# One residual tile per unit, added to in place, and a reordered opening in a planned macaron block (feed-forward, attention, feed-forward) on one Trainium2 core

## The chip, the cores and the metric

The kernel runs on 1 core of one Trainium2 chip. The metric is device time in microseconds (us) of one execution; lower is better. Times that are compared are medians of several runs. A profiled execution gives the trace: what each engine did and when. The engines are PE (TensorE, matrix products), DVE (VectorE), ACT (ScalarE), POOL (GpSimd) and SP (SyncE, which here only issues DMAs). Each engine executes its own queue of instructions in the order in which they were written; an instruction that waits holds up all behind it on that engine.

## The reference

The input x is 32 sequences of 256 tokens of 128 values. The block is

```python
x = x + 0.5 * ffn(layernorm(x))
x = x + attention(layernorm(x))
x = x + 0.5 * ffn(layernorm(x))
```

`ffn` takes the 256 values [x, -x] through three dense layers of widths 512, 512 and 128; the weights are signs (+1 or -1, from boolean arrays k0, k1, k2), each layer is scaled by a scalar (s0, s1, s2), and the first two are followed by `relu(h) * 2`. `attention` has 16 heads of 8 values: Q, K and V projections with biases, softmax of the scaled scores over the 256 tokens of the sequence, the weighted sum of V, and then a layernorm with gamma and beta of (context + its own input).

## The kernel before, in words

Two sequences make a unit, so there are 16 units of 512 tokens; a half of a unit is one sequence. For each unit the kernel runs `first` (the first feed-forward), `norm_attn` and `project` (layernorm, and Q, K, V), `maxima` and `shift` for each half (scores, whose row maxima DVE takes, are made once; the maxima are then written into Q as additional rows by DMA), `weigh` and `context` for each half (the scores are made again, ACT takes the exponential, PE multiplies by V, the layernorm follows), and `second` (the second feed-forward and the store). The last unit runs `second` by halves. Values that need more than float16 are split in two float16 parts, a high one that ACT writes and a low one that DVE writes (or, as below, ACT and POOL).

None of this is issued in program order. Every operation is recorded as a node with an engine, an estimated cost, the keys that it reads and writes, and a rank, which is the unit's number times UNIT = 16 plus an offset of its stage: B0 for the first feed-forward, BA and BP for the attention's norm and projections, BW for the weighing, B1 for the second feed-forward. `_Plan.simulate` then plays the five engines against each other and gives each free engine the ready node of the lowest rank. On PE, feed-forward nodes may run ahead of the scores by at most SKIP ranks (SKIP0 while the rank is below UNTIL); they are what fills PE between scores. The order that comes out is written as fixed instruction queues. The constants do not change the arithmetic, only that order.

A relief rule: an evacuation of PSUM by DVE may be handed to ACT, which writes a float32 tile `full` (two buffers), and POOL, which finishes it, if DVE is backed up by more than BIAS allows. For the sum at the end of a feed-forward, ACT wrote instead into the destination tile itself.

Tiles that matter here: `x` (the unit's input, 4 buffers), `x1` (after the first feed-forward, 7), `x2` (after attention, 4), `x3` (the result, 2); `vaug` and `ks`, three constant buffers each for V and K, which POOL fills with blanks (`blanks`), the ones in V being a copy of `scale`, known only after `projections` has bounded the weights; `xT`, the normalised and turned input of a feed-forward. A unit below QF is turned by PE and then copied by ACT and DVE (`quick`), the others by a DMA transpose on SP after POOL has normalised them. PSUM has two buffers for scores, one for the context, three for all else.

Lines that the steps below use: 368 (a dense product as one 128-row matmul), 371 (the same as four matmuls of 32 columns), 542/543 (statistics on DVE), 544/546 (variance and its power -0.5 on POOL), 551 (quick normalisation on DVE), 571/572 (the high and low parts of a turned tile), 607/608 (high and low parts after a relu), 610/605 (the relief by ACT and POOL), 660 (the residual sum on DVE), 661/662 (the same on ACT and POOL), 767/778 (scores for the maxima, and the maxima on DVE), 835/847 (scores again, and the exponential on ACT), 817 (the context product), 888 (the sum after attention).

Of the kernel before, what the change touches and what calls it, by code (L numbers as in the profile page):

```python
# [53 lines left out]
PT, NHL, NX, NX1, NX2, NXN = 5, 3, 4, 7, 4, 5  # L55

QF, QK = 1, 1
# [7 lines left out]
B0, BA, BP, BW, BV, B1 = -34, -12.145, -7.563, 13, 4, 42.5  # L65

RUSH, AHEAD = 0.302, 5.298

SKIP0, SKIP, UNTIL = 30.226, 7.856, 12.452

WAIT = 0.101
# [3 lines left out]
TURN = 0.1  # L75
# [4 lines left out]
BIAS = 0.471  # L80
# [18 lines left out]
class _Node:  # L99
    __slots__ = ("n", "eng", "cost", "emit", "rank", "kind", "rows", "lag", "needs", "then", "bufs", "count", "avail", "start", "tiling", "alt")  # L100


class _Plan:
# [11 lines left out]
    def op(self, eng, cost, emit, r=(), w=(), rank=0.0, kind="D", rows=0, lag=None, alt=None):  # L115
# [3 lines left out]
        x.then, x.avail, x.start = [], 0.0, None  # L119
# [25 lines left out]
    def simulate(self):  # L145

        free = [0.0] * 5
# [6 lines left out]
        heapq.heappush(events, (0.0, 0, None))  # L154
# [94 lines left out]
        def relief(now, best):  # L249

            nonlocal left
            for x in sorted((x for x in ready[DVE] if x.alt and x.avail <= now + 1e-9), key=lambda x: (x.rank, x.n)):
# [9 lines left out]
                y.n, y.eng, y.cost, y.emit, y.rank, y.kind, y.rows, y.lag, y.alt, y.tiling = x.n, ACT, act, evict, x.rank, "D", 0, None, None, "D"  # L262
                y.needs, y.then, y.bufs, y.count, y.avail, y.start = [], [x], [source, temp], 0, 0.0, None
# [21 lines left out]
        while left:  # L285
# [8 lines left out]
            while again:  # L294
                again = False
                for eng in range(5):
                    if free[eng] > now + 1e-9 or not ready[eng] and eng != ACT:
                        continue
                    if eng == PE:
                        group = choose(now)  # L300
                    else:
                        can = [x for x in ready[eng] if x.avail <= now + 1e-9 and fits(x)]
                        best = min(can, key=lambda x: (x.rank, x.n)) if can else None
                        if eng == ACT:
                            best = relief(now, best) or best
                        group = [best] if best else None
                    if group:
                        begin(group, now)
                        again = True
# [28 lines left out]
def tile_macaron(ctx: ExitStack, tc: tile.TileContext, x, Wq, bq, Wk, bk, Wv, bv, gamma, beta, k0, k1, k2, s0, s1, s2, out):  # L338
# [50 lines left out]
    op(ACT, 0.25, lambda: nc.scalar.copy(ident16, ident), r=["ident"], w=["ident16"], rank=-500)  # L389

    def weights():
# [11 lines left out]
        op(ACT, 0.53, lambda: nc.scalar.dma_start(out=k0s.t, in_=k0.rearrange("(c p) f -> p c f", p=P)), w=[k0s], rank=-900, lag=3.2)  # L403
        for i, src in enumerate((s0, s1, s2)):
            op(SP, 0.47, lambda i=i, src=src: nc.sync.dma_start(out=raw[:, i : i + 1], in_=src.partition_broadcast(P)),
               w=[("raw", i)], rank=-899, lag=2.6)
        op(ACT, 0.53, lambda: nc.scalar.dma_start(out=k1s.t, in_=k1.rearrange("(c p) f -> p c f", p=P)), w=[k1s], rank=-899, lag=4.2)
        op(ACT, 0.53, lambda: nc.scalar.dma_start(out=k2s.t, in_=k2.rearrange("(c p) f -> p c f", p=P)), w=[k2s], rank=-898, lag=4.6)
        raws = [("raw", i) for i in range(3)]
        v = lambda cost, emit, r, w: op(DVE, cost, emit, r=r, w=w, rank=-800)  # L410
# [3 lines left out]
        v(0.6, lambda: nc.vector.tensor_tensor(kd.t, k0s.t[:, 0, :], k0s.t[:, 1, :], ALU.subtract), [k0s], [kd])  # L414
# [10 lines left out]
        v(0.4, lambda: nc.vector.tensor_scalar(w2, k2s.t, 2.0, -1.0, ALU.mult, ALU.add), [k2s], ["w2"])  # L425
        v(0.1, lambda: nc.vector.tensor_tensor(sab, raw, sgn, ALU.mult), [*raws, "sgn"], ["sab"])
        v(0.1, lambda: nc.vector.tensor_tensor(fac, sab[:, 0:1], sab[:, 1:2], ALU.mult), ["sab"], ["fac"])
        v(0.1, lambda: nc.vector.tensor_tensor(fac, fac, raw[:, 2:3], ALU.mult), ["fac", *raws], ["fac"])
        v(0.1, lambda: nc.vector.tensor_scalar(fac, fac, 8.0, None, ALU.mult), ["fac"], ["fac"])
# [9 lines left out]
    def projections():  # L439
# [16 lines left out]
        v = lambda cost, emit, r, w, rank=-600: op(DVE, cost, emit, r=r, w=w, rank=rank)  # L456
# [20 lines left out]
        for i in range(2):  # L477
            op(POOL, 0.5, lambda i=i: permute(br[:, i, 1, :], br[:, i, 0, :], nc.gpsimd.tensor_copy), r=[("br", i)], w=[("brp", i)], rank=-590)
        op(PE, 0.2, lambda: nc.tensor.transpose(bp.t, bound, ident), r=["bound", "ident"], w=[bp], rank=B0 + 2.1)
        v(0.2, lambda: nc.vector.tensor_reduce(top[:, 0:1], bp.t, AX.X, ALU.max), [bp], ["top"])  # L480
        v(0.1, lambda: nc.vector.tensor_scalar(top[:, 1:2], top[:, 0:1], 320.0, 1e-30, ALU.mult, ALU.max), ["top"], ["top"])
        op(POOL, 0.5, lambda: nc.gpsimd.tensor_tensor(top[:, 2:3], top[:, 1:2], nhalf[0:3, 0:1], ALU.pow), r=["top", "nhalf"], w=["top"], rank=-600)
# [3 lines left out]
        op(PE, 0.2, lambda: nc.tensor.matmul(sp.t, ones, diag, start=True, stop=True), r=["ones", "diag"], w=[sp], rank=B0 + 2.2)  # L486
        v(0.1, lambda: nc.vector.tensor_scalar(scale, sp.t, 2.0**13, None, ALU.mult), [sp], ["scale"])
        for i in range(3):
            op(ACT, 0.22, lambda i=i: nc.scalar.activation(ws[:, i, :], ws[:, i, :], AF.Identity, scale=scale[:, i : i + 1]), r=[("ws", i), "scale"], w=[("ws", i)], rank=-600)
# [9 lines left out]
        op(PE, 0.7, turn, r=[*wss, "ident", ("brp", 0), ("brp", 1), "ones"], w=[pw], rank=B0 + 2.3)  # L499
        for i in range(2):  # L500
            op(ACT, 0.4, lambda i=i: permute(wT[:, i, :], pw.t[:, i, :], nc.scalar.copy), r=[pw], w=[("wT", i)], rank=-600)
        op(ACT, 0.22, lambda: nc.scalar.copy(wT[:, 2, :], pw.t[:, 2, :]), r=[pw], w=[("wT", 2)], rank=-600)
        v(0.1, lambda: nc.vector.tensor_tensor(bs, pw.t[:, 3, 0:2], scale[:, 0:2], ALU.mult), [pw, "scale"], ["bs"])
        wTs = [("wT", i) for i in range(3)]
        op(ACT, 0.4, lambda: nc.scalar.copy(wqkv[:, :, 0, :], wT), r=wTs, w=["wqkv0"], rank=-600)
# [9 lines left out]
    def blanks():  # L515
        for j in range(NV):
            rank = -500 if j == 0 else (j - 1) * UNIT * 0.5
# [8 lines left out]
        op(POOL, 0.95, lambda: nc.gpsimd.memset(zero.t.bitcast(F32), 0.0), w=[zero], rank=-501)  # L526
        op(SP, 0.4, lambda: nc.sync.dma_start(out=nought, in_=zero.t), r=[zero], w=["nought"], rank=-500, lag=2)
# [31 lines left out]
    def turned(xn, tag, name, n, rank, quick):  # L559
# [3 lines left out]
        if quick:  # L563
            pt = psum([P, n * P], f"t{name}")

            def turn():
                for t in range(n):
                    nc.tensor.transpose(pt.t[:, bass.ts(t, P)], xn.t[:, t, :], ident)

            op(PE, 0.11 * n, turn, r=[*xns, "ident"], w=[pt], rank=rank)  # L570
            op(ACT, 0.1 * n + 0.1, lambda: nc.scalar.copy(xT.t[:, 0, :], pt.t), r=[pt], w=[(xT, 0)], rank=rank)
            op(DVE, 0.15 * n, lambda: nc.vector.tensor_tensor(xT.t[:, 1, :], pt.t, xT.t[:, 0, :], ALU.subtract), r=[pt, (xT, 0)], w=[(xT, 1)], rank=rank)
        else:
# [5 lines left out]
               r=[(hl, 0), (hl, 1)], w=[(xT, 0), (xT, 1)], rank=rank, lag=3.5)  # L579
        return xT  # L580

    xs, x1s, x2s, xns, qs, xTs, nms, cxs = {}, {}, {}, {}, {}, {}, {}, {}

    def load(u):
        xs[u] = b = buf(io, [P, NT, D], F32, "x", NX, f"x_{u}")
        rank = u * UNIT + B0 - UNIT if u else -1000
        if u == 0:
            for s, (e, eng) in enumerate(((SP, nc.sync), (ACT, nc.scalar))):
                op(e, 0.5, lambda s=s, eng=eng: eng.dma_start(out=b.t[:, 2 * s : 2 * s + 2], in_=xu[u][:, s]), w=[(b, 2 * s)], rank=rank, lag=2.5)
            return  # L590
        op(SP, 0.47, lambda: nc.sync.dma_start(out=b.t.rearrange("p (b c) d -> p b c d", b=2), in_=xu[u]), w=[(b, 0), (b, 2)], rank=rank, lag=2.5)
# [20 lines left out]
    def ffn(key, srcs, dst, n, rank, span):  # L612
# [11 lines left out]
        for m in range(NF):  # L624
# [6 lines left out]
            op(PE, step, layer0, r=["w0", (xT, 0), (xT, 1)], w=[ph], rank=at(i), kind="F")  # L631
# [15 lines left out]
        for t in range(n):  # L647

            def layer2(tiling, t=t):
# [7 lines left out]
        of = lambda: src.t[:, part : part + n]  # L657
        dsts = [(dst, t) for t in (range(0, n, 2) if n == NT else (0,))]
        reads = [(src, part)] + ([(src, part + 2)] if n == NT else [])
        op(DVE, 0.08 + w / 870, lambda: nc.vector.scalar_tensor_tensor(dst.t, po.t, fac, of(), ALU.mult, ALU.add), r=[po, "fac", *reads], w=dsts, rank=at(i),  # L660
           alt=(0.09 + w / 1040, lambda: nc.scalar.activation(dst.t, po.t, AF.Identity, scale=fac), po, dst,
                0.1 + w / 455, lambda: nc.gpsimd.tensor_tensor(dst.t, dst.t, of(), ALU.add)))
        return dsts

    def first(u):
        rank = u * UNIT + B0
        norm_ffn(("ffn0", u), (xs[u], 0), NT, rank - AHEAD, u < QF)
        x1s[u] = buf(io, [P, NT, D], F32, "x1", NX1, f"x1_{u}")
        ffn(("ffn0", u), (xs[u], 0), x1s[u], NT, rank, UNIT)

    def second(u, b):
        n, part = (NT, 0) if b is None else (2, 0)
        src = x2s[u, b]
        rank = u * UNIT + B1 + (b or 0) * UNIT / 2
        norm_ffn(("ffn1", u, b), (src, part), n, rank - AHEAD, u >= NU - QL)
        t = buf(io, [P, n, D], F32, "x3", 2, f"x3_{u}_{b}")
# [266 lines left out]
```

## Time and profile before

| | |
|---|---|
| median of 3 runs | 703.95 us (700.01 to 705.64) |
| the profiled execution's own time | 698.52 us |
| its span, first to last instruction | 696.7 us |
| mean granted TensorE clock | 0.995 |
| DVE busy | 598.9 us (86%), 1224 instructions |
| ACT busy | 531.4 us (76%), 782 instructions |
| POOL busy | 453.7 us (65%), 580 instructions |
| DMA | 46.95 MB, mean 67 GB/s |

Busy time is an average over stages with different limits, so the stages are read separately: an opening until the first scores, a ramp in which attention starts, a long middle in which first feed-forwards, attention and second feed-forwards of different units overlap, a ramp in which no first feed-forwards are left, and the tail after the last context product.

### The profile page before, as it was taken

Reading aid. Unit: us, or ns where it says so; the run is one execution under the profiler, and the core shown is the slowest. Engines: PE = TensorE matmul, PEld = TensorE weight load, DVE = VectorE, ACT = ScalarE, POOL = GpSimd, SP = SyncE. Lnnn points to the kernel's source line nnn. Section 1 sums busy time; section 2 is a strip of 40 time slices with the busy share of each in tenths; the row PEclk is TensorE's granted clock in tenths of the full one; section 3 lists DMA queues with packets and bytes.
Section 4 is the critical chain, followed back from the end, with each engine's and each line's share of the span. In section 5 each row is a group of like instructions: output and inputs, shape, how many; then the busy total and the mean of one; then the engine's idle time right before and its main releaser. Section 6 shows DMA issues by size and latency. Waiting matters only on the chain.

```text
span 696.7 us, 29746 instructions
## 1 busy us (share of the span) xinstructions
PE 648.1 (93%) x13033; PEld 326.6 (47%) x13033; DVE 598.9 (86%) x1224; ACT 531.4 (76%) x782; POOL 453.7 (65%) x580
## 2 busy tenths in 40 slices
PE   1999889899999999999999999999999999788997
PEld 0444444345455444545455454545445454343446
DVE  5679898888989898998989898988989799888785
ACT  2545778887888797887789787887889777776873
POOL 7756869684883959759596858766486746553110
PEclk9999999999999999999999999999999999998999
DMA  5242352224223142413323241423213052401000
GB/s 140 46 118 67 82 109 66 71 41 103 65 60 92 20 133 34 117 38 73 94 46 106 35 134 35 108 30 71 66 32 105 19 119 34 94 5 34 4 17 31
DMA packets 80454, 46.95 MB, mean 67 GB/s; under 512 B 51618, under 2 KB 75684, under 8 KB 80324
## 3 DMA queue, kind: packets, MB, share of 16 engines
q1 hardware_dynamic: 78852, 44.46, 27.0%
q8 instruction: 102, 1.67, 1.0%
q10 hardware_dynamic: 1472, 0.59, 0.3%
q14 instruction: 28, 0.23, 0.1%
HBM read 20.25 MB, written 13.24 MB: 48 GB/s over the span
## 4 chain that ended last, share of the span: by engine, by line
PE 69%; DVE 18%; ACT 5%; DMA 4%; issue 3%; SPq 1%; POOL 1%; ACTq 0%
PE p_None L371 15%; PE p L371 15%; PE cx L817 14%; DVE nm L778 8%; PE sc L835 7%; PE p L368 6%; PE p_None L368 4%; ACT pt L847 3%; PE nat L767 2%; DMA x<-in_L_attn_x_dram 2%; PE tp L861 2%; PE pq L371 2%; DVE mt L789 1%; PE pv L371 1%; DVE h1l L608 1%
## 5 line engine op out<-in xcount | busy, mean ns | idle before, releaser
L847 ACT ACTIVATE pt<-sc,esc 128x1024 f32<-128x1024 f32 x256 | 285.0, 1116 | 73.9 <-PE nat L767 58.5
L778 DVE TENSOR_REDUCE nm<-nat 128x4 f32<-128x1024 f32 x256 | 310.7, 1217 | 34.6 <-PE nat L767 30.4
L817 PE MATMUL cx<-pt,vaug 128*32 128x256 f32 x2048 | 145.4, 384 | 0.4 <-issue 0.2
L371 PEld LDWEIGHTS <-w 128*32 128x32 f16 x3808 | 93.8, 96 | 89.8 <-issue 32.7
L835 PE MATMUL sc<-Q,ks 32*128 32x256 f16 x1024 | 105.1, 274 | 11.6 <-ACT pt L847 11.5
L767 PE MATMUL nat<-ks,Q 32*128 32x256 f16 x1024 | 101.2, 273 | 3.0 <-DVE nm L778 1.9
L817 PEld LDWEIGHTS cx<-pt,vaug 128*32 128x32 f32 x2048 | 63.5, 110 | 51.1 <-issue 13.5
L371 PE MATMUL p<-h1h,w 128*32 128x512 f16 x792 | 80.3, 382 | 0.0
L371 PE MATMUL p<-h1l,w 128*32 128x512 f16 x792 | 79.6, 379 | 0.0
L371 PE MATMUL p_None<-h1h_None,w 128*32 128x512 f16 x712 | 71.2, 382 | 0.2
L371 PE MATMUL p_None<-h1l_None,w 128*32 128x512 f16 x712 | 70.7, 379 | 0.0
L835 PEld LDWEIGHTS <-ks 32*128 32x128 f16 x1024 | 32.0, 92 | 78.4 <-issue 74.0
L607 ACT ACTIVATE h2h<-p 128x512 f16<-128x512 f32 (+1 forms) x72 | 41.1, 571 | 24.1 <-PE p L368 12.4
L608 DVE SCALAR_TENSOR_TENSOR h2l<-p,h2h 128x512 f16<-128x512 f32 (+1 forms) x64 | 41.8, 653 | 15.7 <-ACT h2h L607 15.4
L368 PEld LDWEIGHTS <-w 128*128 128x128 f16 x368 | 34.6, 99 | 37.2 <-issue 11.9
L883 POOL TENSOR_TENSOR y<-y,axn 128x256 f32<-128x256 f32 x28 | 20.4, 730 | 45.9 <-DVE y L881 34.2
L607 ACT ACTIVATE h1h<-p 128x512 f16<-128x512 f32 (+1 forms) x72 | 39.5, 576 | 14.2 <-PE p L368 9.4
L767 PEld LDWEIGHTS <-Q 32*128 32x128 f16 x1024 | 31.5, 92 | 36.5 <-issue 36.2
L607 ACT ACTIVATE h2h_None<-p_None 128x512 f16<-128x512 f32 x60 | 35.8, 597 | 10.6 <-PE p_None L368 7.5
L608 DVE SCALAR_TENSOR_TENSOR h2l_None<-p_None,h2h_None 128x512 f16<-128x512 f32 x47 | 32.1, 682 | 7.0 <-ACT h2h_None L607 6.9
L371 PE MATMUL p_None<-xT_None,w 128*32 128x512 f16 x480 | 34.9, 389 | 2.6 <-DMA xT_None<-hl_None 1.7
L542 DVE BATCH_NORM_STATS2 st_f<-x 128x6 f32<-128x128 f32 x128 | 31.3, 273 | 6.7 <-DMA x<-in_L_attn_x_dram 6.5
(160 smaller groups left out, 1380.0 us busy)
## 6 DMA issues: line engine op xcount, KB each, us to landing
dr<-qkhl SPq DMA_DIRECT2D x32, 256.0 KB
Q<-dr SPq DMA_DIRECT2D x48, 128.0 KB
ks<-dr SPq DMA_DIRECT2D x48, 128.0 KB
x<-in_L_attn_x_dram SPq DMA_DIRECT2D x15, 256.0 KB
out_dram<-x_None SPq DMA_DIRECT2D x15, 256.0 KB
Q<-nought SPq DMA_DIRECT2D x16, 128.0 KB
dm<-mr SPq DMA_DIRECT2D x32, 16.0 KB
Q<-dm SPq DMA_DIRECT2D x32, 16.0 KB
```

What stands on the lines that cost most here:

```text
L368: nc.tensor.matmul(to, w, of, start=start, stop=stop)
L371: nc.tensor.matmul(to[32 * r : 32 * r + 32], w[:, 32 * r : 32 * r + 32], of, start=start, stop=stop)
L542: op(DVE, 0.195, lambda t=t, st=st: nc.vector.bn_stats(st.t, of()[:, t, :]), r=[srcs[t // 2]], w=[st], rank=rank)
L607: op(ACT, 0.09 + w / 1280, lambda: nc.scalar.activation(hi.t[:, m, :], ps.t, AF.Relu), r=[ps], w=[(hi, m)], rank=rank)
L608: op(DVE, 0.08 + w / 985, lambda: nc.vector.scalar_tensor_tensor(lo.t[:, m, :], ps.t, 0.0, hi.t[:, m, :], ALU.max, ALU.subtract), r=[ps, ( ...
L767: nc.tensor.matmul(nat.t[:, ii, qc, :], Q.t[32 * r : 32 * r + 32, g, b * S + qc * P : b * S + qc * P + P], K[32 * r : 32 * r + 32, g, b * ...
L778: op(DVE, 1.141, lambda g=g, pr=pr, nat=nat: nc.vector.tensor_reduce(nm.t[:, :, 2 * pr : 2 * pr + 2, g].rearrange("p q i -> p i q"), nat.t ...
L817: nc.tensor.matmul(cx.t[32 * r : 32 * r + 32, g // 2, :], V[:, 2 * b + kc, 4 * (g // 2) + r, 16 * (g % 2) : 16 * (g % 2) + 32], pts[g, r / ...
L835: nc.tensor.matmul(sc.t[:, ii, kc, :], K[32 * r : 32 * r + 32, g, b * S + kc * P : b * S + kc * P + P], Q.t[32 * r : 32 * r + 32, g, b * S ...
L847: op(ACT, 1.012, lambda pt=pt, sc=sc: nc.scalar.activation(pt.t, sc.t, AF.Exp, scale=esc), r=[sc, "esc"], w=[pt], rank=rank - RUSH)
L861: nc.tensor.transpose(tp.t[:, qc, 8 * c : 8 * c + 8, :].rearrange("p h n -> p (h n)"), cxT.t[:, c, bass.ts(qc, P)], ident)
L883: op(e, cost, lambda: eng.tensor_tensor(y.t, y.t, xn.t[:, 2 * b : 2 * b + 2, :], ALU.add), r=[(xn, 2 * b), (xn, 2 * b + 1)], w=[(y, 0)], r ...
```

## The change

The unit's input tile is kept for the unit's whole life: there are 16 tiles `x0` to `x15`, one buffer each, and `x1`, `x2` and `x3` go. Each residual is added into the tile in place, and the store reads it. Where the relief rule takes a residual sum, ACT now writes it into a `full` tile, shared with the relief of the relu, and POOL adds that to the unit's tile.

In the opening: the blanks get later ranks; the transfer of s0 goes from SP to ACT and ahead of k0; unit 1 is loaded on ACT's queue, ahead of k2, and the other units two units of rank ahead instead of one; unit 0's normalisation gets a rank of -950, ahead of the preparation of the attention weights, which gets ranks behind the start of unit 0; unit 1 is `quick` too (QF = 2); and the quick turn is made in two halves. Planner constants differ (among them SKIP, UNTIL, AHEAD, RUSH, BIAS, S1), and nodes whose rank is over 37.851 ahead of PE's head are held back. HOLD is zero, so the clause that uses it does nothing.

```diff
-PT, NHL, NX, NX1, NX2, NXN = 5, 3, 4, 7, 4, 5
+PT, NHL, NXN = 5, 3, 5
-QF, QK = 1, 1
+QF, QK = 2, 1
-B0, BA, BP, BW, BV, B1 = -34, -12.145, -7.563, 13, 4, 42.5
-RUSH, AHEAD = 0.302, 5.298
-SKIP0, SKIP, UNTIL = 30.226, 7.856, 12.452
-WAIT = 0.101
+B0, BA, BP, BW, BV, B1 = -34, -12.449, -7.379, 13, 4, 42.542
+S0, S1 = 0.0, -1.082
+BB = 2.143
+RUSH, AHEAD = 0.378, 4.629
+SKIP0, SKIP, UNTIL = 30.226, 3.003, 20.423
+FAR = 37.851
+HOLD = (0, 0.0, 0.0)
+WAIT = 0.12
-TURN = 0.1
+TURN = 0.108
-BIAS = 0.471
+BIAS = 0.6
...
-        free = [0.0] * 5
+        free = [0.0, 0.8, 0.7, 0.3, 0.7]
...
-                        can = [x for x in ready[eng] if x.avail <= now + 1e-9 and fits(x)]
+                        far = max(B0, next((g[0].rank for g in line[done:] if g), 1e9)) + FAR
+                        can = [x for x in ready[eng] if x.avail <= now + 1e-9 and x.rank <= far and fits(x)]
...
-        op(ACT, 0.53, lambda: nc.scalar.dma_start(out=k0s.t, ...), w=[k0s], rank=-900, lag=3.2)
-        for i, src in enumerate((s0, s1, s2)):
...
+        for i, (src, e, eng) in enumerate(((s0, ACT, nc.scalar), (s1, SP, nc.sync), (s2, SP, nc.sync))):
...
-            rank = -500 if j == 0 else (j - 1) * UNIT * 0.5
+            rank = j * UNIT + BP - 12
...
-            op(PE, 0.11 * n, turn, r=[*xns, "ident"], w=[pt], rank=rank)
+            for a in range(0, n, 2):
...
+                op(PE, 0.22, turn, r=[*xns[a : a + 2], "ident"], w=[(pt, a)], rank=rank)
...
-        xs[u] = b = buf(io, [P, NT, D], F32, "x", NX, f"x_{u}")
-        rank = u * UNIT + B0 - UNIT if u else -1000
+        xs[u] = b = buf(io, [P, NT, D], F32, f"x{u}", 1, f"x_{u}")
...
+        e, eng, rank = (ACT, nc.scalar, -898) if u == 1 else (SP, nc.sync, (u - 2) * UNIT + B0)
...
-        op(DVE, 0.08 + w / 870, lambda: nc.vector.scalar_tensor_tensor(dst.t, po.t, fac, of(), ALU.mult, ALU.add), r=[po, "fac", *reads], w=dsts, rank=at(i),
-           alt=(0.09 + w / 1040, lambda: nc.scalar.activation(dst.t, po.t, AF.Identity, scale=fac), po, dst,
-                0.1 + w / 455, lambda: nc.gpsimd.tensor_tensor(dst.t, dst.t, of(), ALU.add)))
+        full = buf(work, [P, w], F32, "full", 2, "full")
+        to = lambda: src.t[:, part : part + n]
...
+        op(DVE, 0.08 + w / 870, lambda: nc.vector.scalar_tensor_tensor(to(), po.t, fac, to(), ALU.mult, ALU.add), r=[po, "fac"], w=dsts, rank=at(i),
+           alt=(0.09 + w / 1040, lambda: nc.scalar.activation(full.t.rearrange("p (t d) -> p t d", d=D), po.t, AF.Identity, scale=fac), po, full,
+                0.1 + w / 455, lambda: nc.gpsimd.tensor_tensor(to(), to(), full.t.rearrange("p (t d) -> p t d", d=D), ALU.add)))
...
-        norm_ffn(("ffn0", u), (xs[u], 0), NT, rank - AHEAD, u < QF)
+        norm_ffn(("ffn0", u), (xs[u], 0), NT, rank - AHEAD if u else -950, u < QF)
...
-        rank = u * UNIT + B1 + (b or 0) * UNIT / 2
+        rank = u * UNIT + B1 + S1 * u / (NU - 1) + (b or 0) * UNIT / 2
...
-        op(e, cost, lambda: eng.tensor_tensor(x2.t[:, part : part + 2], z.t, x1.t[:, 2 * b : 2 * b + 2, :], ALU.add), r=[*zs, (x1, 2 * b)], w=[(x2, part)], rank=rank)
+        op(e, cost, lambda: eng.tensor_tensor(x.t[:, part : part + 2], x.t[:, part : part + 2], z.t, ALU.add), r=zs, w=[(x, part)], rank=rank)
```

## The prediction

> **What bounds the kernel now.** I read busy time by stage first, since the share over the whole span (PE 93%) hides where the other 7% lies. The columns are the stage, its length, then the busy us of PE, its weight loads, DVE, ACT and POOL, the granted clock, the DMA share and GB/s.
>
> ```profile
> 0.00:50.00 50.00, 33.89 (x200) 17.36 (x201) 33.46 (x115) 22.71 (x45) 34.18 (x56) 1.00 0.38 96
> 50.00:90.00 40.00, 35.59 (x805) 17.13 (x805) 35.91 (x59) 26.04 (x43) 28.71 (x29) 1.00 0.34 90
> 90.00:130.00 40.00, 35.38 (x705) 17.43 (x697) 34.56 (x74) 32.23 (x45) 29.40 (x37) 1.00 0.38 85
> 130.00:170.00 40.00, 37.91 (x846) 19.34 (x843) 35.91 (x72) 32.26 (x47) 28.64 (x36) 1.00 0.27 56
> 170.00:570.00 400.00, 394.06 (x8590) 197.45 (x8580) 358.86 (x697) 331.46 (x482) 288.72 (x361) 1.00 0.30 71
> ...
> 610.00:650.00 40.00, 35.58 (x592) 15.54 (x584) 34.12 (x60) 28.68 (x38) 14.64 (x20) 0.91 0.07 17
> 650.00:697.00 47.00, 40.85 (x591) 24.43 (x590) 30.62 (x88) 28.02 (x47) 5.99 (x13) 1.00 0.06 19
> ```
>
> PE idles 16.1 us in the opening, 11.1 in the first ramp (50 to 170), 5.9 in the 400 us of the middle, 9.5 in the second ramp (570 to 650; its first half is PE 34.91 of 40) and 6.1 in the tail. PE is the bound in the middle, and the rest can only be won at the ends.
>
> Next the chain of waits over the opening (start, us, what):
>
> ```profile
> 0.72 2.70 DMA x<-in_L_attn_x_dram
> ...
> 4.75 1.38 POOL vaug L518
> 6.13 0.97 POOL rs_f L546
> ...
> 9.34 5.38 DMA x<-in_L_attn_x_dram
> 14.75 0.49 DVE st_f L542 x2
> ...
> 15.88 0.59 DVE xT L572
> 16.51 2.29 PE p L368 x5
> ```
>
> Unit 0's own data were there at 3.4, but its normalisation waited for blanks on POOL, and then its low turned part (L572) stood on DVE behind the statistics of unit 1, whose load landed at 14.7. PE worked on the first layer in earnest from 16.51.
>
> Last the timeline of PE in the second ramp:
>
> ```profile
> 631.24 0.26 PE L835 MATMUL sc<-Q,ks 32*128 32x256 f16 x1 [1.27 <-ACT pt L847]
> 632.40 0.36 PE L767 MATMUL nat<-ks,Q 32*128 32x256 f16 x1 [0.90 <-DVE nm L778]
> 633.13 3.07 PE L817 MATMUL cx<-pt,vaug 128*32 128x256 f32 x15
> ```
>
> Scores have little work between them there, PE idles 1.27 and 0.90 us, and then 15 context matmuls take 3.07 us where 16 take 1.00 elsewhere in the chain: a slow clock (granted 0.63 to 0.69 from 630 to 640).
>
> **The change part by part.** The changed kernel's queues can be read without running it.
>
> *Arithmetic.* Nearly nothing changes in amount: per 128x512 product 496 on each of h1h and h1l in both. A four-piece product costs PE four spacings of 0.054, a whole one 0.217, so the form does not matter. Changes between the three array shapes fall from 559 to 545; a change from columns to rows costs 0.33-0.22 = 0.11 us, so 1.5 us go. But more filler now stands ahead of the last context product: PE work up to it, added by spacings and shape changes, is 647.6 against 647.1, so +0.5 net. In the tail from there on 1.7 us less is left, which buys nothing: the chain from the last context through L861, y, z and L551 took 11 us beside 9.7 us of PE work. Zero, bounds 0 and -1.
>
> *One tile.* The in-place sums write the same shapes; their earlier readers are ancestors anyway, so no new wait of that kind. Loads no longer wait for a buffer. DVE waited for x 6.5 us in all, 2.5 for unit 0 and 3.0 at 14.7 (counted below); the rest, 1.0, is hidden in PE's middle. Zero, bounds 0 and -1. The shared `full` is a rival.
>
> *Opening.* POOL: four memsets now follow each other (0.94, 1.37, 0.94, 1.38), ending at 5.8, then both variances and powers of unit 0 (0.19 twice, 1.01, 0.70) end by 7.9; before, the second power ended at 9.99. DVE: k0 is issued one DMA (0.45) later on ACT, so the difference of the signs (0.69) ends near 5.7, then the sign chain, w0 and a piece of w1 (0.17, 0.16, 0.49, 0.3, 0.48) to 7.3, four L551 (0.33 each, the second pair behind w2, 0.5), the weight-norm product (0.54) and two half turned parts (0.42): about 11.2. The two new waits are on ACT's queue: the load of unit 1 waits until a DMA slot is free again (that of x, 3.4), and k2 behind it for a scalar's (by 5). Behind these stand the table load (1.28), the w1 casts (2.22), then the high turned parts; the casts need the sign chain (6.7) in any case, so this is covered by 0.4 us, and every us beyond that is paid in full. So PE starts at 11.2 instead of 16.51. Then DVE has unit 1's statistics (1.35) and the bound (0.56) before the first low part, but PE is slow as well: spacing 0.43 from 16.51 on, 0.217 from 21.9, which is 5.4 us after the restart (the clock column reads 1.00 throughout; I go by the spacing). I take the same 5.4 us; then PE is at 4.0 us of its work at 17.1, against 22.5 before. Unit 1, now turned by PE, adds to DVE four L551 and two halves (2.2 us) just when its first layer is wanted: 0.8. The second Q/K product stands 0.43 later in PE's queue. The DMAs of Q and K are as before in number and order (dr to scores: 42.3 to 50.9), and PE work before the first score is 29.9 in both. So the first score comes 22.5-17.1-0.8 = 4.6, and with 0.1 for the stalls no longer met, 4.7 us earlier, less at most the 0.43. Blanks of the third buffer move behind unit 2's normalisation on POOL; the DMA that next writes that K comes at 92 us. **-4.7**, bounds -3 (PE starts a us or two later: k2 late) and -6.
>
> The ramp to full clock can be weighed against the Trainium skill, "TensorE: Matmul & The Clock Gate", "What's actually happening": half rate until the array has been busy for one window of some 3.4 us. By that the opening would be worth -5.7, an estimate; the row shows 5.4 us, with gaps in it. Against the change speaks the Trainium skill, "SBUF — State Buffer", "Who interferes with whom": a DVE operation in a two-port mode and a GpSimd operation exclude each other for a whole instruction. The trace agrees: L551 took 1.14 us and w2 1.15 while a 0.95 us memset ran at 7.76. A memset now follows the powers at about 9, beside the last L551; if it costs 0.8 us there, the opening is worth -3.9.
>
> *Ramps.* I added PE's work per score step. The steps at 629.58 and 631.24 lie 1.66 apart, others there up to 1.9, so 1.75 is the pace that DVE and ACT allow. Work short of that: first 64 maxima, 6.2 us before and 7.0 after; last 40, 7.9 and 7.4. Together **+0.3**. DVE's own work, by its rows, falls by 2.1 us over the first 65 maxima and by 3.4 over the last 40 (relief moves it to ACT), where DVE is busy 34 to 36 of 40; I take **-1.0**, bounds 0 and -5.5, nearer zero since PE waits for the exponential as often as for DVE. Against it, at the 41st maximum PE has 4.1 us less work behind it: bound +4.
>
> *The slow clock.* 633.1 to 638.6 lost 2.1 on the context, 0.9 on a 16-piece layer (1.90 against 0.98) and 0.1 on scores: 3.1. It came at the end of eight thin steps (1.0 to 1.5); the new queue has four (0.64, 1.39, 1.02, 0.75) and then 2.67 and 3.8. I take half, **-1.5**, bounds -3 and +3.
>
> **Sum.** -4.7+0.5+0.3-1.0-1.5 = -6.4. The profiled execution took 698.52 (span 696.7 plus 1.8), so 692.1. The median of the runs is 0.78% above it; times 692.1/698.52 = 0.991 it gives 697.5.
>
> **The rivals.**
> - *Both ends gain* (0.22). For: DVE's 5.5 us and the whole slow clock go. Against: equal thin steps. -4.7-5-3 = -13: 691.
> - *The opening is handed back in the first ramp* (0.20). For: six waits of 0.67 to 0.76 of scores for the exponential between 75 and 130, where PE will have 4 us less filler; the work kept back must then be done in PE's saturated middle. Against: the thin-step sums. -6.4+4 = -2.4 or less: 701.5. Here also goes that the opening does not come early, weights or k2 being late: up to 704.
> - *Slower: ACT stuck behind `full`* (0.08). 14 residual sums now take one of its two buffers, 77 writes in place of 57, and 33 of them wait for POOL instead of 19; exponentials queue behind them on ACT, and PE's scores behind those. If POOL's own queue (L662 1.27, a predecessor 1.16) is in the way, each of 14 costs up to 2.4, and PE's slack absorbs about half: -6.4+17 = +10: 714. It decides from six such waits on. Against: in 57 writes ACT never waited for POOL.
>
> **How the numbers follow.** The forecast has 0.50, its own range 693 to 701. Not faster than 689 (the rival's 691 less part of the spread of the runs, 2) and not over 704 (no gain) leaves out the slow rival and a little: 689 to 704. A measurement of this kernel can tell about 1%, 7 us, from no change; that is 696.9, just below the forecast: half of its chance (0.25) and the first rival (0.22) make 0.47 faster, 0.45 is within, 0.08 slower.
>
> **What would show it.** The first layer's steady matmuls near 11.2 and the first score near 46.2; the L572 halves ahead of unit 1's statistics; PE idle of 11 us in the first 120 us after that; no granted clock below 0.9 after 600; no wait of ACT for POOL at `full`. I am wrong if the first score is not 3 us earlier, or if PE idles over 10 us in the middle.

## The result, and the profile after

The median of the changed kernel is 693.5 us (four runs, 692.43 to 695.02), that of the kernel before beside it 704.57 (700.01 to 705.64): a ratio of 0.986, 95% interval 0.981 to 0.991. The change made the kernel faster by some 1.4%.

The profiled execution of the changed kernel took 695.02 us with a span of 693.2. It was the slowest of its four, while the profiled execution before (698.52) was faster than all its timed runs. So the two traces are only 3.5 us apart, where the medians are 11 apart, and what follows explains those 3.5 us best.

First the stages of the changed kernel again: stage, length, busy us of PE, its weight loads, DVE, ACT and POOL, the granted clock, the DMA share and GB/s.

```profile
0.00:50.00 50.00, 36.89 (x220) 18.22 (x224) 36.79 (x125) 23.47 (x48) 34.02 (x56) 1.00 0.41 107
50.00:90.00 40.00, 35.33 (x810) 17.00 (x801) 38.52 (x67) 27.99 (x44) 24.25 (x25) 1.00 0.30 77
90.00:130.00 40.00, 33.94 (x548) 15.67 (x548) 33.14 (x68) 29.84 (x41) 30.97 (x41) 0.87 0.31 66
130.00:170.00 40.00, 39.21 (x879) 20.68 (x882) 35.91 (x73) 33.64 (x50) 32.09 (x41) 1.00 0.28 73
170.00:570.00 400.00, 392.07 (x8818) 202.19 (x8810) 359.05 (x695) 334.61 (x487) 289.96 (x360) 1.00 0.31 71
...
610.00:650.00 40.00, 34.01 (x570) 15.68 (x562) 33.40 (x66) 28.93 (x37) 16.64 (x23) 0.96 0.12 20
650.00:694.00 44.00, 36.62 (x568) 23.35 (x560) 27.81 (x76) 24.83 (x45) 5.93 (x12) 1.00 0.06 20
```

In the opening PE is busy 3.0 us more than before (33.89). The first ramp now has a slow clock (0.87), and the second has less of one (0.96 against 0.91). In the middle PE idles 7.9 us instead of 5.9.

Stages with fixed times hide where work arrives sooner. A better ruler are the starts of DVE's row maxima, of which every kernel here has 256: the opening ends at the first, the first ramp at the 65th, the middle at the 217th, and the rest is the second ramp with the tail. The table holds all kernels of this study (lengths in us of one profiled execution each; the sums are the spans to 0.1 us):

| kernel | opening | first ramp | middle | second ramp and tail | ratio to before (95%) |
|---|---|---|---|---|---|
| before | 51.3 | 137.9 | 373.1 | 134.4 | |
| changed | 49.7 | 138.3 | 373.4 | 131.8 | 0.986 (0.981 to 0.991) |
| changed, again | 48.7 | 136.9 | 374.1 | 132.7 | 0.989 (0.986 to 0.993) |
| tile and clause alone | 51.4 | 134.8 | 377.6 | 138.5 | 1.008 (1.005 to 1.011) |
| constants alone | 54.5 | 139.8 | 374.8 | 130.7 | 1.005 (1.001 to 1.008) |
| opening alone | 50.9 | 136.4 | 372.5 | 134.3 | 0.998 (0.996 to 1.001) |
| all but the opening | 55.1 | 142.5 | 373.5 | 129.9 | 1.003 (1.000 to 1.006) |
| more score matmuls | 49.0 | 143.1 | 374.6 | 135.7 | 1.005 (1.003 to 1.008) |
| `pm` later | 48.3 | 136.5 | 375.7 | 131.4 | 0.988 (0.984 to 0.992) |
| blanks later | 48.7 | 136.9 | 374.1 | 131.1 | 0.988 (0.984 to 0.992) |
| UNTIL put back | 49.4 | 139.6 | 381.3 | 130.6 | 0.999 (0.997 to 1.001) |
| SKIP put back | 49.6 | 136.6 | 376.7 | 139.7 | 1.001 (0.999 to 1.003) |
| UNTIL, blanks later | 50.2 | 141.3 | 380.7 | 131.1 | 1.002 (1.000 to 1.004) |
| WAIT, TURN put back | 48.0 | 137.5 | 381.6 | 134.4 | 1.003 (1.001 to 1.005) |

The ratios are of medians, each against the kernel before on the same chip.

The chain of waits over the opening answers to the one shown of before (start, us, what):

```profile
1.62 4.50 DMA k0s<-in_L_ffn_k_dram
...
8.29 0.75 DVE fxn L566 x2
...
9.77 1.41 DVE fxn L566 x2
...
12.91 0.34 DVE xT L589
13.30 2.29 PE p L383 x5
```

Unit 1's load and the blanks are gone from it. The first layer (L383, line 368 before) runs steadily from 13.30 instead of 16.51. It is now held by the landing of k0, at 6.12, and then by DVE: two of the quick normalisations (L566, line 551 before) take 1.41 us where one alone takes 0.33.

The timeline of PE in the second ramp, where the clock fell before:

```profile
627.99 0.26 PE L849 MATMUL sc<-Q,ks 32*128 32x256 f16 x1 [0.33 <-ACT pt L861]
628.80 0.26 PE L781 MATMUL nat<-ks,Q 32*128 32x256 f16 x1 [0.55 <-DVE nm L792]
...
629.13 1.74 PE L831 MATMUL cx<-pt,vaug 128*32 128x256 f32 x16
```

The waits are 0.33 and 0.55 instead of 1.27 and 0.90, but a slow context product still follows, of 1.74 us.

### The profile page after: what moved, and what is told of

It reads as the page before. It is cut to its first block, busy times and chain, and to the rows that moved or that the text cites. A ratio compares the mean times of both kernels' runs of the same rounds, so it can differ in the third digit from the quotient of the medians.

```text
span 693.2 us, 29847 instructions
## 1 busy us (share of the span) xinstructions
PE 644.7 (93%) x13082; PEld 330.4 (48%) x13082; DVE 600.2 (87%) x1227; ACT 536.6 (77%) x792; POOL 458.8 (66%) x585
## 4 chain that ended last, share of the span: by engine, by line
PE 70%; DVE 15%; ACT 9%; issue 3%; DMA 2%; SPq 1%; ACTq 0%; POOL 0%
PE p_None L386 17%; PE cx L831 15%; PE p L386 15%; PE sc L849 7%; DVE nm L792 5%; ACT pt L861 5%; PE p L383 4%; PE nat L781 3%; PE p_None L383 2%; PE tp L875 2%; DVE mt L803 2%; PE pv L386 1%; ACT qkhl L728 1%; DVE qkhl L730 1%; PE pq L383 1%
## 5 line engine op out<-in xcount | busy, mean ns | idle before, releaser
L386 PEld LDWEIGHTS <-w 128*32 128x32 f16 x4048 | 103.5, 96 | 97.6 <-issue 31.0
L831 PE MATMUL cx<-pt,vaug 128*32 128x256 f32 x2048 | 139.0, 389 | 0.0
L386 PE MATMUL p<-h1h,w 128*32 128x512 f16 x860 | 87.0, 383 | 0.1
L386 PE MATMUL p<-h1l,w 128*32 128x512 f16 x860 | 86.3, 380 | 0.0
L386 PE MATMUL p_None<-h1h_None,w 128*32 128x512 f16 x800 | 80.6, 382 | 0.9 <-ACT full L628 0.8
L831 PEld LDWEIGHTS cx<-pt,vaug 128*32 128x32 f32 x2048 | 59.0, 110 | 47.0 <-issue 16.7
L386 PE MATMUL p_None<-h1l_None,w 128*32 128x512 f16 x800 | 80.4, 379 | 0.3 <-issue 0.3
L383 PEld LDWEIGHTS <-w 128*128 128x128 f16 x308 | 29.6, 100 | 29.4 <-issue 10.5
L626 DVE SCALAR_TENSOR_TENSOR h1l<-p,h1h 128x512 f16<-128x512 f32 (+1 forms) x59 | 38.1, 655 | 4.5 <-ACT h1h L625 4.2
L625 ACT ACTIVATE h1h_None<-p_None 128x512 f16<-128x512 f32 x60 | 34.5, 605 | 5.4 <-PE p_None L386 5.3
```

The source lines that it names most:

```text
L383: nc.tensor.matmul(to, w, of, start=start, stop=stop)
L386: nc.tensor.matmul(to[32 * r : 32 * r + 32], w[:, 32 * r : 32 * r + 32], of, start=start, stop=stop)
L625: op(ACT, 0.09 + w / 1280, lambda: nc.scalar.activation(hi.t[:, m, :], ps.t, AF.Relu), r=[ps], w=[(hi, m)], rank=rank)
L626: op(DVE, 0.08 + w / 985, lambda: nc.vector.scalar_tensor_tensor(lo.t[:, m, :], ps.t, 0.0, hi.t[:, m, :], ALU.max, ALU.subtract), r=[ps, ( ...
L831: nc.tensor.matmul(cx.t[32 * r : 32 * r + 32, g // 2, :], V[:, 2 * b + kc, 4 * (g // 2) + r, 16 * (g % 2) : 16 * (g % 2) + 32], pts[g, r / ...
```

## The experiments

### Which part carries the gain

Four kernels take the change apart. In the first the residual tile comes with the clause on nodes far ahead, and all else is as before:

```diff
-        xs[u] = b = buf(io, [P, NT, D], F32, "x", NX, f"x_{u}")
+        xs[u] = b = buf(io, [P, NT, D], F32, f"x{u}", 1, f"x_{u}")
...
+                        far = max(B0, next((g[0].rank for g in line[done:] if g), 1e9)) + FAR
```

> The residual tile alone, added to in place, with the old opening and the old constants; only the clause that holds back nodes far ahead of PE's head comes with it, since the tiles no longer limit how far work runs ahead. Theory A (the tile itself is free): first score at 50.9 as before, DVE's waits for x change nothing on PE, and the time is within 0.4% of the kernel before. Theory B (loads without a wait are worth something): PE idles 2 us less in the middle and the time falls by 0.5% or more. Theory C (ACT stuck behind `full`): waits of ACT for POOL at `full`, and the time rises by 0.5% or more.

The second has the constants, the clause and the planner's details alone:

```diff
-B0, BA, BP, BW, BV, B1 = -34, -12.145, -7.563, 13, 4, 42.5
+B0, BA, BP, BW, BV, B1 = -34, -12.449, -7.379, 13, 4, 42.542
-SKIP0, SKIP, UNTIL = 30.226, 7.856, 12.452
+SKIP0, SKIP, UNTIL = 30.226, 3.003, 20.423
...
```

> The planner's constants, the clause for nodes far ahead and the sort order of relief nodes alone; old tiles, old opening (first score 50.9). Theory A (the constants carry the gain at the second ramp): the stretch from the 217th maximum to the 256th, 88.8 us in the kernel before, falls to about 84 as in the changed kernel, and the time falls by 0.6 to 1.0%. Theory B (any new plan lands within some 3 us): the stretch stays over 87 and the time is within 0.4% of the kernel before.

The third has the opening alone (weights, projections, blanks, halves, QF = 2, the loads):

```diff
-QF, QK = 1, 1
+QF, QK = 2, 1
...
-            rank = -500 if j == 0 else (j - 1) * UNIT * 0.5
+            rank = j * UNIT + BP - 12
...
```

> The reordered opening alone, with old tiles and constants. Theory A (the opening's 1.6 us at the first score are kept to the end): first layer steadily at 13.3, first score at 49.3, and the time falls by 0.2 to 0.5%. Theory B (handed back in the first ramp): the 41st maximum is not earlier than 130, and the time is within 0.2%. If the opening carries most of the change's gain, the time falls by 1% or more.

The fourth is the changed kernel with that opening undone, so the first and second together:

> The changed kernel with its opening undone: tiles and constants as changed, first score at 50.9. Theory A (the parts add): 0.2 to 0.5% above the changed kernel's 693.5, so 695 to 697, ratio to the kernel before 0.987 to 0.990. Theory B (the opening is handed back): 693.5 within 0.2%. If the constants without the opening bring nothing, the ratio is over 0.995.

Measured: 704.43, 702.69, 698.57 and 702.62 us beside 700.75 of the kernel before. No part is worth the gain, and three of four make the kernel slower. The fourth's ratio, 1.003, is the last case of its expectation: without the opening the constants bring nothing.

- The tile itself costs nothing. Constants without and with it give PE, DVE, ACT and POOL the very same queues and the same time, 702.69 and 702.62. What made the first kernel slower is that the clause changed the plan: put into the kernel before without the tile, the clause alone gives the same four queues as this kernel. The middle and the end became 4.5 and 4.1 us longer. The time is theory C's, but its reason is not: ACT has no wait for POOL at `full`.
- The constants shorten the stretch from the 217th to the 256th maximum from 88.9 to 83.3 us, as theory A asked, and the whole end by 3.7 (134.4 to 130.7). They lose 5.2 up to the 65th maximum and 1.6 in the middle: without the new opening the first maximum comes at 54.5. So the time rose where theory A had it fall. In the chain of that kernel, three low parts of unit 1's feed-forward stand on DVE (1.80 us at 36.02) in the middle of the normalisation for unit 0's attention.
- The opening alone gains 0.4 us at the first maximum and 2.7 at the end of the span; the time falls by 0.2%, within its interval. Theory A's first score at 49.3 did not come (49.99), and with the 41st maximum at 128.8 theory B's did not either. With the new constants the same opening brings the first maximum from 55.1 to 49.7 and 48.7, by 5.4 to 6.4 us, and the ratio from 1.003 to 0.989. The parts don't add.
- They don't add in the plans either. The end that the planner itself computes (`self.end` in `run`) is 675.7 us before and 667.0 in the changed kernel, but 680.6 with tile and clause, 674.2 with the constants (with or without the tile) and 674.6 with the opening alone.

### The slow clock

The changed kernel was run again beside the next three, as their reference.

> The changed kernel again, beside the next three on one chip, as their reference. Median 693.5 before; both theories expect the same ratio of about 0.986 to the kernel before, and a granted clock of about 0.5 again at 90 to 93 and 100 to 107, since its queues are fixed.

It gave 693.44 beside 700.14. But the clock fell at other times: at 99.0 and 126.3 in the first ramp, where the first execution has 90.1 and, for twice as long, 100.3. The records of the granted clock show why. In every execution it changes on a grid of 3.41 us (in the first execution: full for 71.68 us, half for 3.41, full for 6.83, half for 6.83, full for 522.24), and the grid lies elsewhere each time. So the next windows lie along the grid. The changed kernel's first execution, columns as above:

```profile
83.25:86.66 3.41, 1.93 (x41) 0.85 (x36) 3.41 (x7) 2.86 (x5) 1.15 (x1) 1.00 0.19 36
86.66:90.07 3.41, 1.66 (x28) 0.76 (x17) 3.41 (x11) 2.27 (x3) 1.03 (x2) 1.00 0.71 202
90.07:93.49 3.42, 3.16 (x56) 1.79 (x59) 3.24 (x11) 1.32 (x2) 2.87 (x4) 0.50 0.62 175
93.49:96.90 3.41, 2.36 (x62) 1.19 (x52) 2.50 (x5) 2.92 (x6) 2.17 (x5) 1.00 0.50 144
96.90:100.31 3.41, 1.59 (x33) 0.91 (x32) 2.16 (x3) 2.23 (x3) 3.41 (x5) 1.00 0.01 1
100.31:103.73 3.42, 3.13 (x36) 0.93 (x32) 2.60 (x7) 2.58 (x4) 3.34 (x5) 0.50 0.52 119
```

Each window has the clock at 1.00 or at 0.50 from end to end. After PE was busy 1.66 and 1.59 us of 3.41, the next window is at half; after 1.93 and 2.36 it is not.

To fill such windows, the next kernel has four more score matmuls behind 34 score steps of the two ramps:

```diff
+                        for i in range(4 if warm and qc and ii else 0):
+                            q = 2 * pr
+                            nc.tensor.matmul(warm.t[:, i % 2, :], Q.t[32 * q : 32 * q + 32, ...], K[32 * q : 32 * q + 32, ...], start=True, stop=True)
```

> The changed kernel with four more score matmuls, in one row tile and into a PSUM tile that nobody reads, behind the score step of maxima 19 to 32 and 237 to 256. Theory A (an idle PE brings the clock down: PE was busy 2.83 us of 84 to 90 and 3.14 of 94 to 100, and the granted clock was near 0.5 right after, at 90 to 93 and 100 to 107, and again at 628 to 634): no 2-us window under 0.9 after 60 us; the 113th maximum, 306.6 in the changed kernel, comes 3 to 5 us earlier, and the time falls by 0.4 to 0.8%. Theory B (the clock falls for another reason): the same stretches stay near 0.5. Theory C (the clock does not set the end of the stretch, or the extra matmuls cost as much): clock at 1.00, but the 113th maximum within 1 us of 306.6 and the time within 0.2%.

It took 704.55, 1.6% more than the changed kernel beside it. No theory said that. The first ramp became 6.2 us longer, and the clock fell there all the same, once for three windows and once for one. Around the first of these:

```profile
92.72:96.14 3.42, 1.66 (x23) 1.04 (x23) 3.14 (x7) 1.71 (x3) 2.61 (x4) 1.00 0.59 156
96.14:99.55 3.41, 3.41 (x36) 1.41 (x30) 1.23 (x1) 1.11 (x1) 3.33 (x6) 0.50 0.22 44
99.55:102.96 3.41, 2.98 (x24) 1.54 (x26) 2.45 (x2) 2.54 (x3) 2.21 (x3) 0.50 0.00 0
```

Most windows were filled (2.43 and 3.04 in the two ahead), but in one PE waited for DVE and ACT, the added matmuls waited with it, and 1.66 us let the clock fall. Then the added matmuls took twice as long. In the second ramp the clock stayed at 1.00, but the end grew by 3 us all the same. So the cause of theory A holds, as far as the windows show it, and the cure costs more than the illness.

### Waits of PE that a plan can't see

The regular new wait of PE in the middle is for the maxima's operations on DVE. The next kernel issues their transposes two groups of PE later, and leaves the rest of the plan alone:

```diff
+            if group[0].kind == "C" and group[0].cost == 0.12:
+                held.append([group, LATE])
+                continue
```

> The changed kernel with the same plan, but the transposes of the maxima (L809) issued two groups later on PE. Theory A (the planner's cost of the two operations on `mt`, 0.20 and 0.12 against 0.32 and 0.52 in the trace, puts PE in front of a wait of some 0.6 us per unit, 5.2 us in the 400 us of the middle): that wait falls under 1.5 us, PE is busy 395 or more of the 400, and the time falls by 0.3 to 0.6%. Theory B (the wait is taken over by the next one, since DVE sets the pace of the maxima): L809's wait goes, but PE's busy time in the middle stays at 392 to 393 and the time within 0.2%.

The waits of PE from 170 to 570 (us in total, times, longest), of the changed kernel again:

```profile
PE pm L809 <- DVE mt L803: 5.3, 9, 0.8
PE p L386 <- issue: 1.8, 1, 1.8
```

and with the transposes later:

```profile
PE p L401 <- issue: 2.0, 1, 2.0
PE sc L864 <- DVE nm L807: 1.7, 6, 0.3
PE pv L401 <- DVE qkhl L745: 1.3, 2, 1.0
PE pq L401 <- DVE qkhl L745: 0.6, 1, 0.6
```

The wait of 5.3 us is gone, PE's busy time there is 392.24 against 391.39, and the time is 693.29 against 693.44: theory B. At these places PE now waits for DVE's next result instead, as if DVE set the pace. One thing blurs this in the trace: the clock was at half there from 252.16 to 255.57, after a gap of 2.0 us with no cause in the profile, and between the 89th and the 97th maximum this kernel falls back by 1.8 us against the changed kernel again. That one has three windows at half clock as well, but none in the middle. So the verdict rests on the medians.

### The blanks and the opening

```diff
-            rank = j * UNIT + BP - 12
+            rank = j * UNIT + BP - 12 if j != 1 else 5
```

> The changed kernel with the blanks of the second V and K buffers moved behind the start of unit 0's first layer. Theory A (the blanks on POOL hold up the opening, once by queueing ahead of unit 0's variance, which came at 5.83 with the statistics ready at 4.7, and once by running beside the normalisation on DVE): first layer steadily by 11.5 instead of 13.3, first score at 47.5 instead of 49.3, 0.2 to 0.3% of the time. Theory B (the landing of k0 at 6.1 and the chain of signs hold it): the first layer not before 12.8 and the first score within 0.5 us of 49.3.

The first layer started at 12.74 (13.17 in the changed kernel again), the first maximum came at 48.7 as there, and the time was 692.78, the same within the interval. The number is nearly theory B's (it had 12.8 as the earliest start), the reason is neither's. Unit 0's powers on POOL did come earlier (4.79 and 5.87, against 6.37 and 7.39 in the changed kernel), and k0's difference was done at 7.19. But then the moved blanks met the normalisation. POOL's timeline:

```profile
9.17 1.37 POOL L533 MEMSET vaug<- 128x1536 f32 x1
10.49 0.94 POOL L534 MEMSET ks<- 128x1024 int32 x1
```

and DVE's in the same execution:

```profile
8.51 3.01 DVE L566 TENSOR_SCALAR fxn<-x,mv_f,rs_f 128x128 f32<-128x128 f32 x2
9.04 2.48 DVE L589 TENSOR_TENSOR xT<-t,xT 128x256 f16<-128x256 f32 x1
...
9.49 2.29 DVE L440 TENSOR_SCALAR w<-k2s 128x512 f16<-128x512 uint8 x1
```

The second of the two normalisations and all behind it on DVE ended only when the second memset did: 3.01 us for two normalisations of 0.33 each. That fits the rule of the Trainium skill, "SBUF — State Buffer", "Who interferes with whom", that DVE and GpSimd share a pair of ports under an exclusive lock. The page has the lock for one instruction; here DVE stood still through both memsets, 2.3 us. Moved out of one queue, the blanks blocked another.

### Which constants

UNTIL lets the feed-forward run 30 ranks ahead at the start; SKIP bounds that later. Two kernels put one of them back, a third puts UNTIL back and moves the blanks too:

```diff
-SKIP0, SKIP, UNTIL = 30.226, 3.003, 20.423
+SKIP0, SKIP, UNTIL = 30.226, 3.003, 12.452
```

> The changed kernel with one constant put back: UNTIL 12.452 in place of 20.423, so the feed-forward stops running 30 ranks ahead earlier. By its queue, PE's work over maxima 1 to 17, 17 to 25 and 25 to 33 is 21.3, 16.2 and 14.4 us, against 26.8, 13.9 and 11.0 in the changed kernel and 23.9, 16.5 and 14.3 in the kernel before; from the 217th maximum on it is the changed kernel's. Theory A (the constants starve PE between the 17th and the 33rd maximum; windows of 3.4 us in which PE is busy half or less bring the clock to a half): no granted window under 0.9 from 60 to 170 us, the 113th maximum 2 to 4 us earlier than in the run of the changed kernel again (304.9), the late part unchanged, and 689 to 691 us, 0.4 to 0.7% less than the changed kernel. Theory B (the work is only shifted and is missing elsewhere in the ramp): within 0.2% of 693.4.

```diff
-SKIP0, SKIP, UNTIL = 30.226, 3.003, 20.423
+SKIP0, SKIP, UNTIL = 30.226, 7.856, 20.423
```

> The changed kernel with one constant put back: SKIP 7.856 in place of 3.003, so that later on the feed-forward may run further ahead of the scores. By its queue the work from the 217th maximum to the end is spread as in the kernel before (35.4 us behind the 256th maximum, 37.4 before, 39.0 in the changed kernel), and maxima 25 to 33 get 14.3 in place of 11.0. Theory A (a short SKIP is what makes the stretch from the 217th to the 256th maximum some 5 us shorter): that stretch goes back from 84 to 88 or more, the first ramp gains 1 to 3, and the time is 695 to 697. Theory B (the late gain comes from other constants): the stretch stays at 84 to 85 and the time is at or under the changed kernel's 693.4.

> The changed kernel with UNTIL at 12.452 and the second buffers' blanks behind the start of unit 0. Theory A (both small gains are real and in different places): under the better of the two alone, 688 to 691. Theory B (the blanks bring nothing): the time of the run with UNTIL alone within 0.15%.

They took 702.94, 703.65 and 704.37 beside 703.12 of the kernel before: each loses the whole gain. With UNTIL back the clock was at half for one window, from 69.7, and then full from 73.1 us to the end, nearly as theory A asked. Yet the first ramp was 2.7 us longer than in the changed kernel again and the middle 7.1. From 124 to 320, PE now waited 5.5 us for `mt` and 2.6 for a low part of Q or K, against 3.6 and none. So the slow clock was not what set the end of the ramp, and my reading of the thin steps fell. SKIP did at the end what theory A said: the stretch from the 217th to the 256th maximum takes 92.5 us with 7.856 put back. In the three other kernels with that value it takes 88.9 to 90.8, and in the eight with 3.003 and no added matmuls 82.5 to 86.5. The extra was larger than expected, 2.6 more went in the middle, and the first ramp gained 0.2 and not 1 to 3, so the time missed theory A's 695 to 697. The third shows that later blanks add nothing.

The last kernel puts back two constants that change nothing but the order:

```diff
-WAIT = 0.12
+WAIT = 0.101
-TURN = 0.108
+TURN = 0.1
```

> The changed kernel with the two smallest constants put back, WAIT 0.101 in place of 0.12 and TURN 0.1 in place of 0.108: the planner's allowance for a short wait of PE and its cost of a change of shape. They alter nothing on the chip but the order. By the queue, PE's work over maxima 1 to 65 and 233 to the end is the changed kernel's within 0.6 us, and 2.5 us move from maxima 65 to 113 into 113 to 217. Theory A (the gain belongs to two things, the work kept back by a short SKIP for the end and the early running ahead by UNTIL): both are there, so 692 to 695, a ratio to the kernel before of 0.986 to 0.990, and the stretch from the 217th to the 256th maximum stays at 84 to 85. Theory B (the gain belongs to the one plan that came out, and a new deal falls back to where most deals lie): 699 to 704, a ratio over 0.994.

It took 702.57 beside 699.66, a ratio of 1.003: theory B. Up to the 113th maximum it keeps pace with the changed kernel (306.3 against 305.1 in the second execution), then it loses 6.2 us up to the 217th: PE is busy 3.5 us more there and idles 2.7 us more. Both things of theory A are in it (the stretch from the 217th to the 256th maximum took 86.5 us, though, and not 84 to 85), and the gain is gone.

The planner's own end is 672.7 us with UNTIL back, 682.8 with SKIP, 672.1 with UNTIL and later blanks and 675.5 with WAIT and TURN. It sets the changed kernel's 667.0 apart from all of them, but it does not order the rest: the plan of 672.1 took 704.37, the opening alone with 674.6 took 698.57.

No kernel here is clearly better than the changed one: moved blanks and later transposes give 692.78 and 693.29 against 693.44, inside the intervals.

## Why the prediction was right, and where it was not

697.5 was forecast, in a range of 689 to 704, and 693.5 came. By its own steps:

- **Opening, -4.7.** The mechanism was right and the size was not: in the two profiled executions the first score came 1.6 and 2.6 us earlier, at 49.3 and 48.3 and not near 46.2. By the prediction's own sign ("if the first score is not 3 us earlier") this step was wrong. The failing term is DVE's, "four L551 (0.33 each, the second pair behind w2, 0.5), the weight-norm product (0.54)", which should have ended at 11.2 with the half turned parts. The pairs took 1.37 and 1.41, w2 1.13 and the product 0.83, while POOL's copies (L490) ran, four in 2.04 us (1.16 in the kernel with later blanks), and then a memset. The contention was weighed, but for the last L551 only. k0's difference ended at 6.83 instead of 5.7, POOL's powers at 8.26 instead of 7.9. Steady matmuls thus began at 13.30, not 11.2. The way to the full clock was misread as well: 21.9 is the next dense product, but the clock's record of the kernel before begins at 20.92, so 4.4 us after the restart and not 5.4; in the changed kernel it took 5.1 and 3.9. The halves did come ahead of unit 1's statistics, as said.
- **One tile, 0.** Right: 702.69 and 702.62 with the same queue on PE. ACT never waited for POOL at `full`, so the slower rival did not come.
- **Middle.** No change was forecast: 373.1 before, 373.4 and 374.1 after, and PE idles 7.9 and 8.6 us of the 400, under the 10 that were named. Right, though plans with one or two constants put back lose 7 us there.
- **The ends: +0.5, +0.3, -1.0 and -1.5, so -1.7.** Both ends together went from 272.3 to 270.1 and 269.5, by -2.1 and -2.7: right in sum. The places were off. The second ramp and tail gave 1.7 to 2.6, the first ramp between +0.5 and -1.0. The slow clock, of which half was to go, halved in the second ramp (6.83 us to 3.41) and appeared in the first. The sign that no granted clock under 0.9 would show after 600 was wrong.
- **From the profile to the median, times 0.991.** This step failed. The trace gave -3.5 and not -6.4; the forecast for the profiled execution was 692.1, and it took 695.02. But the kernel before had run 6 us faster in its profiled execution than its median of 704.57, and the changed kernel ran 1.5 slower than its own. So one error of +2.9 and one of some -7 went against each other, and that the forecast came as near as it did is in part luck. In four further sets the median of the kernel before was 699.7 to 703.1.
- **The rivals.** The opening was not handed back in the first ramp: alone, it gains 0.4 us at the first maximum and 2.6 at the 256th. Both ends did not gain 13.

That the kernel as a whole is 1.1 to 1.4% faster is shown. That this is the sum of its edits is refuted: the planner deals the whole order anew for each change, and of the nine kernels here that have another plan on PE (all but the two with `pm` or the blanks later), none comes below 0.998. What their plans have in common was there to be read before any run: the planner's own end puts the changed kernel 8.7 us below the kernel before, and each of the nine at least 3 us above the changed one. What stays open is why one deal passes the middle in 373 us and another, with the same work to within a per cent, in 381: the trace names the waits (Q and K's low parts, the maxima), not what in the order makes them. From the 65th to the 217th maximum PE is busy 366 to 369 us in the changed kernel and in the three slow deals, but it idles 7.5 and 8.4 us in the one and 12.9 to 14.0 in the others, 8.3 to 12.3 of it for DVE. It is also open why the kernel before varies from 696 to 707 us; the free grid of the clock may be part of it, since a thin stretch falls into one window in one execution and is split over two in another.

## What to carry to other kernels

Where a planner lays out the order, an edit and its constants have one price together and none apart; predict from the queue that came out and from the end that the planner computes for it, and try a change again with the constants nudged before believing that an edit earned its gain. A wait that disappears from PE is worth its time only where PE, and not DVE behind it, sets the next step. Keep long memsets on POOL away from a chain that runs through DVE.

## What the hardware showed

- The clock of PE is decided window by window, on a grid of 3.41 us that starts anywhere. I took PE's busy share in each window from the records of all fourteen profiled executions (40 to 680 us, windows at full clock). Of 13 windows with PE busy under half, 12 were followed by half clock (the other, busy 1.61 us from 249.2 in the changed kernel again, was not, and why is open); of 76 between 0.50 and 0.65, 13; of some 2,500 above 0.65, none. The Trainium skill, "TensorE: Matmul & The Clock Gate", "What's actually happening", has the free-running window, 3413 ns by its figure, and the trace agrees; it says that the clock falls after an idle window, and here windows that were busy for 1.3 to 2.1 us were enough.
- The grid shows at the start too: the first layer ran steadily from 13.30 and 13.17 in two executions of the changed kernel, but the fast clock began at 18.4 and 17.1, and their first maxima differ by 1.0. By these figures 1.2 us more at half clock are worth some 0.6 of it, an estimate; the rest is not explained.
